# Second layer's scans: four of sixteen states turned in place of two, with a second tile of scaled copies and new tables by step

## The chip, the core and the metric

The kernel runs on one core of a Trainium2 chip. The core has a matrix engine (TensorE, in profiles PE for its matmuls and PEld for its weight loads), three engines that work on 128 partitions side by side (VectorE, DVE; ScalarE, ACT; GpSimd, POOL), and a queue that issues DMAs (SyncE, SP). Each runs its own instructions in order and waits for the others by semaphores. The metric is the device time of one execution in microseconds (us), lower is better. The kernel before takes 8835.18 us, the median of three runs (8833.89 to 8835.39).

## What is computed

The program is four layers on a tensor of 2 x 56 x 56 x 128. The change touches the second alone. It splits the 128 channels into four heads of 32 and works through them one after the other, since each head takes the result of the one before as input. The core of a head is a selective scan in four directions:

```
def _selective_scan(xs, dts, A, Bs, Cs, Ds):
    def step(h, inp):
        x_t, dt_t, B_t, C_t = inp
        dA = jnp.exp(dt_t[..., None] * A)
        h = dA * h + (dt_t * x_t)[..., None] * B_t[:, :, None, :]
        y = jnp.einsum('bkdn,bkn->bkd', h, C_t)
        return (h, y)
...
x1 = xx.reshape(B, L, d)
x2 = xx.transpose(0, 2, 1, 3).reshape(B, L, d)
xs = jnp.stack([x1, x2, jnp.flip(x1, 1), jnp.flip(x2, 1)], axis=1)
x_dbl = jnp.einsum('bkld,kcd->bklc', xs, p['x_proj_w'])
dts, Bs, Cs = jnp.split(x_dbl, [DT_RANK, DT_RANK + D_STATE], axis=-1)
```

Here L = 3136 pixels, d = 64 channels, n = 16 states. For each direction, channel and state there is a recurrence over the pixels: h = exp(delta A) h + (delta x) B, and the output sums h C over the 16 states. B and C do not depend on the channel, only on pixel and state; delta (after a softplus) and x do not depend on the state.

## The kernel before, in words

Both images lie side by side: 2 x 64 channels fill the 128 partitions. The pixels of one direction are cut into four quarters of 784 (`QT`), which makes 4 x 4 = 16 groups in a head. A group has 16 steps, one for each state, so a head has 256 steps and the layer 1024. Class `Scans` does this for both layers, with a table of settings from each; the first layer has 1024 steps of the same size in two runs of 512.

One step for state n of a group is:

- `decay` (L381): ACT computes a = exp(A delta).
- the input (delta x) B, in one of three ways. A **direct** state: PE spreads the row of B over all partitions into a PSUM tile named `b` (`spread`, L407, two bf16 matmuls), and DVE multiplies it by `du` = delta x (L479). A **pooled** state: DMAs copy the row to all partitions and POOL multiplies (L498). A **turned** state: `du` has been transposed once a group into `duT` (pixels on the partitions, `turn`, L237), and there B of a pixel is one number of a partition. ACT writes 7 x 2 scaled copies of `duT` for a state (`fan`, L359: seven blocks of 112 pixels, two images) into a tile bT, and PE transposes the seven blocks back into PSUM (`back`, L370).
- `scan` (L401): DVE runs the recurrence over the 784 pixels.
- POOL multiplies h by the row of C, which DMAs have copied to all partitions (p, L495), and PE adds p into the sum in PSUM, `acc` (`add_up`, L421).

For direct and pooled states a lies in PSUM, in one of two slots that the steps take by turns, and h in SBUF. For turned states it is the other way round: a lies in SBUF, and the input takes the slot. So the exponential of step s+1 waits for the scan of step s-1, whose slot it takes, unless s+1 is turned; that one is issued a step earlier still.

The order of all instructions is written out by hand. `emit(s)` issues for step s: ACT's `decay` of s+1 (if not turned), the copy of the state of s-1, `decay` of s+2 if turned, and the scaled copies that stand for s; PE's `back` of s+1; DVE's direct product of s+1; PE's `spread` of s+2; the prepared pieces; DVE's `scan` of s; the DMAs for C of s+3 and for B of s+6 if pooled; POOL's product p of s and, if s+3 is pooled, its input; and PE's additions. Three tables say how much of what stands at which step:

- `adds`: how many additions PE issues at a step, by the step modulo 32.
- `fans`: how the 14 scaled copies of a turned state are dealt out over the six steps before it; the key is the state's step modulo 32.
- `lists`: the pieces that prepare the next two groups during the 32 steps of the present pair, as (offset, place, name). The steps of a pair are counted 16 to 47, so a piece of offset 4 stands at step 20. `short` is the same for the first group of a head (steps 0 to 15, some pieces a little later), in which the groups 1 and 2 are prepared. All groups but the first go in pairs.

The pieces: `rows` (PE, then an ACT copy) projects x; `keep` and `fetch` send the rows to DRAM and back by SP's queue; `band` (ACT) and `rest` (POOL, L202) split the values of B into three bf16 parts; `store` and `spread` bring those by SP's queue to where PE reads them; `across` transposes B for the turned states (PE, ACT); `steps` (PE, ACT) and `soft` (ACT's softplus, which needs another table of functions than the exponential, so that ACT loads tables twice around it) give delta; `copy` (ACT) puts x into PSUM and `times` (DVE, L231) makes `du` from it; `turn` (PE, ACT) makes `duT`. `rows`, `steps`, `across`, `turn` and `copy` use the same single PSUM tile `b` as `spread`; each user waits until the one before has been read.

SP's queue also issues all DMAs for the rows of C and B, in the order of the program. The places in memory that matter: bT and the two `duT` lie in `big[5]`, each 896 columns wide. `big[0]` and `big[1]` are the halves of one tile, `pair`; in this layer `big[0]` holds the gate and the first 1792 columns of `big[1]` hold `prev`, the running result between heads. `run` of the layer runs the scans of a head, then the work between heads.

The tiles for turned states are handed out by turns:

```
self.duT, self.bT = w["turn"][0:2], w["turn"][2:]
...
for i, x in enumerate(x for x in steps if x["n"] in self.turned):
    x["bT"] = self.bT[i % len(self.bT)]
...
def direct(self, x):
    return x["n"] not in self.pooled and x["n"] not in self.turned
```

Of the kernel before, what the change touches and what calls it, by code (L numbers as in the profile page):

```python
# [21 lines left out]
B = 2  # L22
# [3 lines left out]
TP = 112  # L26
NT = L // TP
# [7 lines left out]
class Chip:  # L35


    def __init__(self, ctx, tc):
        self.tc, self.nc = tc, tc.nc
        nc = tc.nc  # L40
        const = ctx.enter_context(tc.tile_pool(name="const", bufs=1))
        self.ident = const.tile([128, 128], F32, name="ident")
        make_identity(nc, self.ident)
        self.eps = const.tile([128, 1], F32, name="eps")
        nc.gpsimd.memset(self.eps, 1e-5)
        self.one = const.tile([128, 1], F32, name="one")
        nc.gpsimd.memset(self.one, 1.0)
        self.ones = const.tile([1, 128], F32, name="ones")
        nc.gpsimd.memset(self.ones, 1.0)
        self.X = const.tile([TP, NT, B, C], F32, name="X")  # L50
        self._turn = 0
# [56 lines left out]
TS = QT // TP  # L108
# [469 lines left out]
def negative_exp(nc, t):  # L578
    nc.scalar.activation(t, t, AF.Exp)
    nc.vector.tensor_scalar_mul(t, t, -1.0)  # L580
# [19 lines left out]
def load(nc, pool, ap, name):  # L600
    t = pool.tile(list(ap.shape), F32, name=name)
    nc.sync.dma_start(t, ap)
    return t
# [232 lines left out]
class Layer1:  # L836
# [4 lines left out]
    D = 32  # L841

    def __init__(self, k, ctx, d, big):
        nc, tc = k.nc, k.tc
        D = self.D
        self.k = k
        wp = ctx.enter_context(k.pool("w1", side="right"))
        W = self.W = {n: load(nc, wp, d["L1_" + n], "L1" + n) for n in (
            "in_w", "taps", "conv_b", "dtb", "A", "Ds", "onw", "onb", "out_w")}

        xp = wp.tile([128, 4, 128], F32, name="xp1")
        dt = wp.tile([128, 4, 128], F32, name="dt1")
        nc.gpsimd.memset(xp, 0.0)
        nc.gpsimd.memset(dt, 0.0)
        for b in range(B):
            r, c = 34 * b, NS * b
            for i in range(2):
                o = r + 2 + NS * i
                nc.sync.dma_start(xp[:, :, 32 * i + c : 32 * i + c + NS], d["L1_xproj"][:, :, o : o + NS])
            nc.sync.dma_start(xp[:, :, 96 + 2 * b : 98 + 2 * b], d["L1_xproj"][:, :, r : r + 2])  # L860
            nc.sync.dma_start(dt[96 + 2 * b : 98 + 2 * b], d["L1_dt"][r : r + 2])
        sel = selection(k, wp, 2)
        R = self.R = {}
        for n in ("vss_skip", "cvm_skip", "final_ln_w", "final_ln_b"):
            t = wp.tile([TP, d["L1_" + n].shape[0]], F32, name="L1" + n)
            nc.sync.dma_start(t, d["L1_" + n].partition_broadcast(TP))
            R[n] = t
        nc.vector.tensor_scalar_add(R["vss_skip"], R["vss_skip"], 1.0)
        negative_exp(nc, W["A"])
        self.diag = wp.tile([128, 9, 128], F32, name="diag1")  # L870
        diagonals(k, self.diag, W["taps"])

        center = wp.tile([128, 128], F32, name="center1")
        nc.gpsimd.memset(center, 0.0)
        nc.gpsimd.memset(center[0:64, 0:64], 1.0 / 64)
        nc.gpsimd.memset(center[64:128, 64:128], 1.0 / 64)
        nc.vector.tensor_tensor(center, k.ident, center, ALU.subtract)
        skip = skips(k, wp, W["Ds"].unsqueeze(2), 1, center)
        self.mean = wp.tile([128, 2], F32, name="mean1")
        nc.gpsimd.memset(self.mean, 0.0)  # L880
        for b in range(B):
            nc.gpsimd.memset(self.mean[64 * b : 64 * (b + 1), b : b + 1], 1.0 / 64)
        self.outs = []
        for n in ("onw", "onb"):
            t = wp.tile([128, B * D], F32, name="out" + n)
            nc.vector.tensor_scalar(t, W["out_w"], W[n], None, ALU.mult)
            self.outs.append(t)

        lnw = wp.tile([B * D, 2], F32, name="lnw")
        for b in range(B):  # L890
            for i, n in enumerate(("ln1_w", "ln1_b")):
                nc.sync.dma_start(lnw[D * b : D * (b + 1), i : i + 1], d["L1_" + n].rearrange("(c o) -> c o", o=1))
        inb = self.inb = wp.tile([128, 2], F32, name="inb")
        with k.pool("pinb", psum=True) as pp:
            ps = pp.tile([128, 2], F32, name="pinb")
            for i in range(2):
                nc.tensor.matmul(ps[:, i : i + 1], lhsT=W["in_w"][:, i, :], rhs=lnw[:, 1:2], start=True, stop=True)
            nc.vector.tensor_copy(inb, ps)
        nc.vector.tensor_scalar(W["in_w"], W["in_w"], lnw[:, 0:1], None, ALU.mult)
        self.prev = big[1][:TP, 0 : NT * B * D].rearrange("p (j b c) -> p j b c", b=B, c=D)  # L900
        self.z, self.row, self.col, self.y = (big[i][:, 0:L] for i in (0, 2, 4, 3))
        self.scans = Scans(k, ctx, 1, [self.row], [self.col], [self.y], {
            "xproj": lambda kd, ci: xp[:, kd, :],
            "dt": lambda kd, ci: dt[:, kd, :],
            "dtb": lambda kd, ci: W["dtb"][:, kd : kd + 1],
            "A": lambda kd, ci, n: W["A"][:, kd, n : n + 1],
            "selB": lambda n: sel[:, n],
            "unused": sel[:, 0:4].rearrange("p n c -> p (n c)"),
            "skip": lambda ci: skip[:, 0],
            "sum": center,  # L910
            "rows": 64,
            "rowC": 32,
            "copies": (0, NS),
            "parts": ((0, 64, 0), (64, 128, NS)),
            "pooled": (1, 6, 9, 14),
            "turned": (3, 11),
            "adds": (0, 2, 2, 0, 0, 1, 2, 1, 1, 1, 1, 2, 1, 1, 1, 0, 3, 1, 0, 0, 0, 1, 2, 1, 1, 1, 2, 0, 1, 1, 1, 1),
            "soon": False,
            "fans": {
                None: (0, 4, 4, 4, 2, 0),  # L920
                3: (0, 10, 4, 0, 0, 0),
                11: (4, 0, 1, 7, 2, 0),
                19: (4, 5, 5, 0, 0, 0),
                27: (5, 1, 3, 2, 3, 0),
            },
            "lists": [
                [
                    (1, 0, "rows", [0, 1]), (2, 2, "keep"), (4, 0, "steps", 0, [0, 1]), (5, 2, "fetch"),
                    (9, 0, "across"), (9, 2, "band", 0), (9, 2, "rest", 0), (10, 2, "band", 1),
                    (10, 2, "rest", 1), (11, 2, "band", 2), (17, 2, "soft", 0), (19, 2, "store"),  # L930
                    (22, 2, "spread"), (23, 0, "copy", 0), (23, 2, "times", 0), (25, 0, "turn", 0),
                ],
                [
                    (12, 0, "rows", [0, 1]), (14, 2, "keep"), (15, 0, "steps", 0, [0, 1]), (17, 2, "soft", 0),
                    (19, 2, "fetch"), (20, 0, "across"), (27, 2, "band", 0), (27, 2, "rest", 0),
                    (28, 0, "copy", 0), (28, 2, "times", 0), (29, 2, "band", 1), (29, 2, "rest", 1),
                    (31, 2, "band", 2), (33, 2, "store"), (35, 2, "spread"), (39, 0, "turn", 0),
                ],
            ],
            "short": [  # L940
                [
                    (1, 0, "rows", [0, 1]), (4, 2, "keep"), (4, 0, "steps", 0, [0, 1]), (5, 2, "fetch"),
                    (6, 2, "soft", 0), (7, 0, "across"), (7, 2, "band", 0), (7, 2, "rest", 0),
                    (7, 2, "times", 0, False), (8, 2, "band", 1), (8, 2, "rest", 1), (9, 2, "band", 2),
                    (9, 2, "store"), (10, 2, "spread"), (12, 0, "turn", 0),
                ],
                [
                    (1, 0, "rows", [0, 1]), (1, 2, "keep"), (4, 0, "steps", 0, [0, 1]), (6, 2, "soft", 0),
                    (7, 0, "across"), (10, 2, "fetch"), (14, 2, "band", 0), (14, 2, "rest", 0),
                    (17, 2, "band", 1), (17, 2, "rest", 1), (19, 2, "band", 2), (20, 2, "store"),  # L950
                    (21, 2, "times", 0, False), (23, 0, "turn", 0), (24, 2, "spread"),
                ],
            ],
            "turn": [
                big[5][:TP, 128 * TS * i : 128 * TS * (i + 1)].rearrange("p (i c) -> p i c", c=128) for i in range(3)
            ],
        }, side="right")

# [1261 lines left out]
```

## Time and profile before

| what | value |
|---|---|
| median of three runs | 8835.18 us |
| the profiled execution, its own time | 8835.43 us |
| its span, first to last instruction | 8833.6 us |
| first layer's scans, two runs of 512 steps | 1184.6 and 1179.8 us |
| second layer's scans, four heads of 256 steps | 638.7, 638.4, 636.6, 636.6 us |
| busy over the whole span: PE, DVE, ACT, POOL | 8003.9, 6756.2, 5217.6, 6844.0 us |
| mean granted clock of TensorE | 0.958 |

The four heads' scans are 2550 us of the span, 29%. The rest (the first layer, the work between heads, both later layers) holds none of the changed instructions. For the whole program the slices of the page show which engine is busy when; each digit is the busy share of a fortieth of the span (221 us) in tenths:

```profile
DVE  8999998999987997998899799821266676665442
ACT  6888876888876776776777677533322222214331
POOL 5999986999986996998799699666577767756551
```

The second layer's heads are the thirteenth to the twenty-sixth slice; the digits that fall to 5 to 7 in DVE's row there are the stretches between heads. In a stretch of scans DVE, POOL and PE are all busy most of the time, so the slices cannot say which of them sets the pace. That is read from the table by stretch, and from what each engine's idle time waited for. In those lines a group reads: line, engine, operation, what it writes and reads, shapes, count | busy us, mean ns of one | idle time of the engine just before them, and who ended it.

### The profile page before, as it was taken

The page shows a single profiled execution, that of the slowest core. Times are in us where ns is not written, and L with a number is a line of the kernel's source. Part 1 is how long each engine was busy: PE and PEld are TensorE (multiplying, and loading weights), DVE is VectorE, ACT ScalarE, POOL GpSimd, SP SyncE. Part 2 cuts the span into 40 slices and gives each one's busy share as a digit, 9 for nine tenths or more (in the row PEclk, how much of TensorE's full clock was granted, in tenths as well). Part 3 has the DMA queues.
Part 4 walks back from the last instruction along what each step waited for, and adds up shares of the span by engine and source line. Part 5 has one row for each costly group of instructions (what it writes and reads, how often), then busy time and mean ns, then how long its engine had stood idle before and what let it go on. Part 6 is the DMA issues. An engine that isn't in the chain of part 4 may idle for free. (4 is left out here: it accounts for less than half of the span.)

```text
span 8833.6 us, 103494 instructions
## 1 busy us (share of the span) xinstructions
PE 8003.9 (91%) x31559; PEld 4877.1 (55%) x31559; DVE 6756.2 (76%) x7017; ACT 5217.6 (59%) x11166; POOL 6844.0 (77%) x4232
## 2 busy tenths in 40 slices
PE   8999999999998888888888888699989989989998
PEld 4555555555554444444444444345578878875555
DVE  8999998999987997998899799821266676665442
ACT  6888876888876776776777677533322222214331
POOL 5999986999986996998799699666577767756551
PEclk9999999999998999999899899799999999989999
DMA  4676654667654884885688488320133333320004
GB/s 145 217 218 213 211 186 128 217 217 213 211 179 109 221 219 118 215 223 161 173 224 216 116 224 219 93 34 3 30 98 106 103 93 106 104 56 8 15 1 139
DMA packets 846617, 1276.69 MB, mean 145 GB/s; under 512 B 182813, under 2 KB 504350, under 8 KB 846058
## 3 DMA queue, kind: packets, MB, share of 16 engines
q1 hardware_dynamic: 846058, 1270.07, 50.7%
q8 instruction: 249, 4.08, 0.2%
q14 instruction: 310, 2.54, 0.1%
HBM read 1230.00 MB, written 46.58 MB: 145 GB/s over the span
## 5 line engine op out<-in xcount | busy, mean ns | idle before, releaser
L495 POOL TENSOR_TENSOR p<-h,c 128x784 f32<-128x784 f32 x2048 | 3763.7, 1864 | 291.8 <-DVE h L401 146.0
L401 DVE TENSOR_TENSOR_SCAN h<-a,state,h 128x784 f32<-128x784 f32 x1200 | 2169.9, 1833 | 2.5 <-ACT a L381 1.6
L421 PE MATMUL acc<-p,center 128*128 128x392 f32 x4096 | 1496.8, 501 | 6.5 <-POOL p L495 6.3
L421 PE MATMUL acc<-p,ident 128*128 128x392 f32 x4096 | 1429.5, 493 | 0.5 <-POOL p L495 0.4
L479 DVE TENSOR_TENSOR h<-du,b 128x784 f32<-128x784 f32 x1152 | 1096.5, 952 | 229.7 <-PE b L407 212.5
L381 ACT ACTIVATE a<-delta,L1A 128x784 f32<-128x784 f32 x896 | 819.8, 915 | 425.0 <-DVE h L401 418.6
L421 PEld LDWEIGHTS acc<-p,ident 128*128 128x128 f32 x4096 | 747.6, 190 | 533.4 <-issue 33.4
L421 PEld LDWEIGHTS acc<-p,center 128*128 128x128 f32 x4096 | 743.0, 193 | 497.1 <-issue 25.0
L1232 POOL TENSOR_TENSOR total<-total,e 128x448 f32<-128x448 f32 (+1 forms) x644 | 734.6, 1141 | 329.1 <-ACT e L1221 289.6
L498 POOL TENSOR_TENSOR h<-du,b 128x784 f32<-128x784 f32 x448 | 831.7, 1857 | 0.0
L1221 ACT ACTIVATE e<-sc 128x448 f32<-128x448 f32 (+1 forms) x700 | 376.9, 542 | 722.8 <-PE sc L1219 594.6
L407 PE MATMUL b<-three,sel 96*128 96x512 bf16 (+1 forms) x2304 | 587.0, 336 | 174.0 <-DVE h L479 102.0
L381 ACT ACTIVATE a<-delta,L0A 128x784 f32<-128x784 f32 x704 | 643.3, 914 | 169.7 <-DVE h L401 165.2
L401 DVE TENSOR_TENSOR_SCAN h<-a,h 128x784 f32<-128x784 f32 x400 | 702.6, 1774 | 3.5 <-ACT a L381 3.1
L359 ACT ACTIVATE X<-X,BT 112x128 f32<-112x128 f32 x2100 | 683.8, 391 | 0.2
L1736 POOL TENSOR_TENSOR u<-u,T 128x1024 f32<-128x1024 f32 x192 | 448.6, 2358 | 265.9 <-DVE u L1734 265.7
L401 DVE TENSOR_TENSOR_SCAN h<-h,state,a 128x784 f32<-128x784 f32 x336 | 618.0, 1839 | 0.0
L1720 ACT ACTIVATE less<-cv 128x512 f32<-128x512 f32 x256 | 152.1, 595 | 612.2 <-PE cv L1698 586.9
L407 PEld LDWEIGHTS <-sel 96*128 96x128 bf16 x2304 | 225.0, 101 | 521.3 <-issue 365.5
L359 ACT ACTIVATE big<-big,BT 112x64 f32<-112x64 f32 x1680 | 444.6, 335 | 0.0
L1732 ACT ACTIVATE T<-T 128x1024 f32<-128x1024 f32 x128 | 135.2, 1056 | 407.4 <-DVE T L1730 279.2
L1837 PE MATMUL pj<-u,Wm 128*128 128x196 f32 (+8 forms) x1536 | 355.6, 385 | 21.2 <-POOL u L1756 11.1
(541 smaller groups left out, 14336.4 us busy)
## 6 DMA issues: line engine op xcount, KB each, us to landing
c<-rows SPq DMA_DIRECT2D x1024, 392.0 KB, 4.0
c<-rows SPq DMA_DIRECT2D x2048, 196.0 KB, 4.0
b<-rows SPq DMA_DIRECT2D x512, 196.0 KB, 4.6
b<-rows SPq DMA_DIRECT2D x192, 392.0 KB, 4.6
wA<-win SPq DMA_DIRECT2D x64, 448.0 KB, 3.9
wB<-win SPq DMA_DIRECT2D x64, 448.0 KB, 6.2
wC<-win SPq DMA_DIRECT2D x64, 448.0 KB, 4.7
wD<-win SPq DMA_DIRECT2D x64, 448.0 KB, 3.8
```

Source lines behind the costliest of these rows:

```text
L359: self.k.nc.scalar.activation(x["bT"][:, i, c0:c1], g["duT"][x["ci"]][:, i, c0:c1], AF.Copy, scale=g["BT"][:, r : r + 1])
L381: self.k.nc.scalar.activation(x["a"], g["delta"][ci], AF.Exp, scale=self.w["A"](g["kd"], ci, x["n"]))
L401: self.k.nc.vector.tensor_tensor_scan(h, a, b, start, ALU.mult, ALU.add)
L407: self.k.nc.tensor.matmul(ps[:, c0:c1], lhsT=self.w["selB"](x["n"]), rhs=x["g"]["three"][:, c0:c1], start=True, stop=True)
L421: nc.tensor.matmul(job["acc"][:, i, 0:392], lhsT=self.w["sum"], rhs=x["p"][:, 392 * i : 392 * (i + 1)], start=False, stop=n == NS - 1,)
L479: nc.vector.tensor_tensor(one["h"], one["g"]["du"][one["ci"]], one["b"], ALU.mult)
L495: nc.gpsimd.tensor_tensor(now["p"], now["h"], now["c"], ALU.mult)
L498: nc.gpsimd.tensor_tensor(three["h"], three["g"]["du"][three["ci"]], three["b"], ALU.mult)
L1221: nc.scalar.activation(e[:n], ps[:n], AF.Exp, scale=scale)
L1232: nc.gpsimd.tensor_tensor(total[:n], total[:n], e[:n], ALU.add)
L1736: nc.gpsimd.tensor_tensor(u[:, :, :, o], u[:, :, :, o], half, ALU.add)
L1837: nc.tensor.matmul(ps[:, lo - c0 : hi - c0], lhsT=Ws[f][:, eo, 3 - r, :], rhs=u[:, b, f, lo - a0 : hi - a0], start=f == 0, stop=f == 1,)
```

## The change

In the second layer's settings the states 7 and 15 join 3 and 11 as turned ones; the pooled ones stay, so eight of sixteen are direct where ten were. A fourth tile is added to `turn`, in the free columns of `big[1]` behind `prev`, so that there are two bT by turns. The tables `adds`, `fans`, `lists` and `short` are new; the pieces are the same, at other steps. No function is changed.

```diff
             "pooled": (1, 6, 9, 14),
-            "turned": (3, 11),
-            "adds": (0, 2, 2, 0, 0, 1, 2, 1, 1, 1, 1, 2, 1, 1, 1, 0, 3, 1, 0, 0, 0, 1, 2, 1, 1, 1, 2, 0, 1, 1, 1, 1),
+            "turned": (3, 7, 11, 15),
+            "adds": (2, 0, 2, 0, 2, 0, 1, 3, 0, 2, 1, 1, 1, 0, 1, 2, 1, 1, 0, 0, 0, 1, 2, 1, 1, 1, 1, 2, 1, 0, 1, 1),
             "soon": False,
             "fans": {
                 None: (0, 4, 4, 4, 2, 0),
-                3: (0, 10, 4, 0, 0, 0),
-                11: (4, 0, 1, 7, 2, 0),
-                19: (4, 5, 5, 0, 0, 0),
-                27: (5, 1, 3, 2, 3, 0),
+                3: (1, 10, 1, 1, 1, 0),
+                7: (3, 9, 0, 2, 0, 0),
+                11: (1, 0, 0, 13, 0, 0),
+                15: (6, 2, 2, 4, 0, 0),
+                19: (0, 6, 0, 4, 4, 0),
+                23: (2, 2, 7, 3, 0, 0),
+                27: (1, 6, 3, 2, 2, 0),
+                31: (0, 5, 5, 4, 0, 0),
             },
             "lists": [
                 [
-                    (1, 0, "rows", [0, 1]), (2, 2, "keep"), (4, 0, "steps", 0, [0, 1]), (5, 2, "fetch"),
-                    (9, 0, "across"), (9, 2, "band", 0), (9, 2, "rest", 0), (10, 2, "band", 1),
-                    (10, 2, "rest", 1), (11, 2, "band", 2), (17, 2, "soft", 0), (19, 2, "store"),
-                    (22, 2, "spread"), (23, 0, "copy", 0), (23, 2, "times", 0), (25, 0, "turn", 0),
+                    (1, 0, "rows", [0, 1]), (5, 0, "steps", 0, [0, 1]), (6, 2, "keep"), (11, 2, "fetch"),
+                    (12, 0, "across"), (15, 2, "band", 0), (15, 2, "rest", 0), (17, 2, "band", 1),
+                    (17, 2, "rest", 1), (20, 2, "band", 2), (21, 2, "store"), (22, 2, "soft", 0),
+                    (23, 0, "copy", 0), (23, 2, "times", 0), (25, 2, "spread"), (28, 0, "turn", 0),
                 ],
                 [
-                    (12, 0, "rows", [0, 1]), (14, 2, "keep"), (15, 0, "steps", 0, [0, 1]), (17, 2, "soft", 0),
-                    (19, 2, "fetch"), (20, 0, "across"), (27, 2, "band", 0), (27, 2, "rest", 0),
-                    (28, 0, "copy", 0), (28, 2, "times", 0), (29, 2, "band", 1), (29, 2, "rest", 1),
-                    (31, 2, "band", 2), (33, 2, "store"), (35, 2, "spread"), (39, 0, "turn", 0),
+                    (13, 0, "rows", [0, 1]), (15, 0, "steps", 0, [0, 1]), (17, 2, "keep"), (22, 2, "fetch"),
+                    (22, 2, "soft", 0), (26, 2, "band", 0), (26, 2, "rest", 0), (29, 0, "across"),
+                    (31, 2, "band", 1), (31, 2, "rest", 1), (31, 0, "copy", 0), (31, 2, "times", 0),
+                    (33, 2, "band", 2), (36, 2, "store"), (40, 2, "spread"), (41, 0, "turn", 0),
                 ],
             ],
             "short": [
                 [
-                    (1, 0, "rows", [0, 1]), (4, 2, "keep"), (4, 0, "steps", 0, [0, 1]), (5, 2, "fetch"),
-                    (6, 2, "soft", 0), (7, 0, "across"), (7, 2, "band", 0), (7, 2, "rest", 0),
-                    (7, 2, "times", 0, False), (8, 2, "band", 1), (8, 2, "rest", 1), (9, 2, "band", 2),
-                    (9, 2, "store"), (10, 2, "spread"), (12, 0, "turn", 0),
+                    (1, 0, "rows", [0, 1]), (1, 2, "keep"), (3, 2, "fetch"), (5, 0, "across"),
+                    (5, 2, "band", 0), (5, 2, "rest", 0), (6, 2, "band", 1), (6, 2, "rest", 1),
+                    (7, 0, "steps", 0, [0, 1]), (9, 2, "band", 2), (9, 2, "store"), (10, 2, "spread"),
+                    (10, 2, "soft", 0), (11, 2, "times", 0, False), (13, 0, "turn", 0),
                 ],
                 [
-                    (1, 0, "rows", [0, 1]), (1, 2, "keep"), (4, 0, "steps", 0, [0, 1]), (6, 2, "soft", 0),
-                    (7, 0, "across"), (10, 2, "fetch"), (14, 2, "band", 0), (14, 2, "rest", 0),
-                    (17, 2, "band", 1), (17, 2, "rest", 1), (19, 2, "band", 2), (20, 2, "store"),
-                    (21, 2, "times", 0, False), (23, 0, "turn", 0), (24, 2, "spread"),
+                    (5, 0, "rows", [0, 1]), (6, 2, "keep"), (9, 2, "fetch"), (9, 0, "steps", 0, [0, 1]),
+                    (10, 2, "soft", 0), (12, 2, "band", 0), (12, 2, "rest", 0), (14, 2, "band", 1),
+                    (14, 2, "rest", 1), (14, 2, "times", 0, False), (15, 0, "across"), (23, 2, "band", 2),
+                    (23, 2, "store"), (23, 0, "turn", 0), (25, 2, "spread"),
                 ],
             ],
             "turn": [
-                big[5][:TP, 128 * TS * i : 128 * TS * (i + 1)].rearrange("p (i c) -> p i c", c=128) for i in range(3)
+                t[:TP, at : at + 128 * TS].rearrange("p (i c) -> p i c", c=128)
+                for t, at in [(big[5], 128 * TS * i) for i in range(3)] + [(big[1], NT * B * D)]
             ],
```

## The prediction, made before the changed kernel was run

> **What bounds the kernel now.** I read the page first: the chain of waits stops after one step (0%), so it says nothing, and the busy shares (PE 91%, POOL 77%, DVE 76%) mix stages. The change touches only the second layer's scans, so the table by stretch comes next, one row for each of the four heads, from its first scan to its last:
>
> ```profile
> core 0: us, PE busy (x) PEld busy (x) DVE busy (x) ACT busy (x) POOL busy (x), PEclk, DMA share, GB/s
> ...
> 2768.82:3407.54 638.72, 549.27 (x1952) 296.28 (x1951) 604.37 (x430) 461.33 (x1060) 594.15 (x349) 0.94 0.80 215
> 3503.69:4142.12 638.43, 548.37 (x1952) 295.19 (x1951) 604.43 (x430) 461.42 (x1060) 596.53 (x350) 0.95 0.80 212
> 4239.57:4876.21 636.64, 548.00 (x1952) 296.15 (x1951) 604.27 (x430) 461.42 (x1060) 594.63 (x349) 0.94 0.80 213
> 4973.51:5610.10 636.59, 547.83 (x1952) 296.16 (x1951) 604.22 (x431) 461.39 (x1060) 594.81 (x350) 0.94 0.79 213
> ```
>
> Mean head 637.6 us: DVE busy 604.3 (95%), POOL 595.0 (93%), PE 548 (86%), ACT 461 (72%). The groups by line for DVE, and the waits of POOL, both in the second head alone:
>
> ```profile
> L401 DVE TENSOR_TENSOR_SCAN h<-a,state,h 128x784 f32<-128x784 f32 x168 | 303.2, 1835 | 0.8 <-POOL h L498 0.8
> L479 DVE TENSOR_TENSOR h<-du,b 128x784 f32<-128x784 f32 x159 | 151.3, 952 | 33.2 <-PE b L407 31.7 <-POOL p L495 0.4
> ```
> ```profile
> POOL p L495 <- PE acc L421: 13.2, 11, 2.0
> POOL p L495 <- DVE h L401: 11.6, 14, 5.3
> ```
>
> DVE's whole idle time in a head (33 us) stands before its direct products and ends with b, the rows that PE spreads into the one PSUM tile `b`. No scan waits for ACT, while ACT itself waits 105 us a head for scans. So DVE sets the pace, its only loss is the shared tile, and POOL has 42 us to spare. Scan starts in this head give 52.0 us for the first group of 16 steps, 42.1 for the second and (4142.1 - 3597.8)/14 = 38.9 for each other. The first group's direct products alone wait 13.7 us; there two later groups are prepared in 16 steps.
>
> Durations on the page include a tail that overlaps the next instruction. For sums I use the distance of starts, read off the order of time in the second head:
>
> ```profile
> 3593.85 2.24 ACT L359 ACTIVATE big<-big,BT 112x64 f32<-112x64 f32 x9
> 3601.55 1.28 ACT L221 ACT_TABLE_LOAD   x1
> 3602.84 1.61 ACT L221 ACTIVATE delta<-delta 128x784 f32<-128x784 f32 x2
> ```
> ```profile
> 3599.54 0.94 DVE L479 TENSOR_TENSOR h<-du,b 128x784 f32<-128x784 f32 x1
> 3600.40 3.58 DVE L401 TENSOR_TENSOR_SCAN h<-a,state,h 128x784 f32<-128x784 f32 x2
> ```
> ```profile
> 3602.30 0.89 PE L370 MATMUL a<-ident,big 112*128 112x112 f32 x7 [0.26 <-DVE h L401]
> 3603.03 0.50 PE L407 MATMUL b<-three,sel 96*128 96x512 bf16 x2
> ```
>
> One product 0.86 us (3600.40 - 3599.54), one scan 1.75, one scaled copy 0.24 (nine in 2.24 less one tail), seven transposes 0.73, one spread 0.33 to 0.5. POOL's starts are 1.81 apart, and its small subtraction takes 0.5.
>
> **The change, part by part.** Per head there are 16 groups. The 32 steps of a pair of groups are counted 16 to 47, as in the tables; those of the first group 0 to 15.
>
> 1. States 7 and 15 are turned instead of direct. DVE loses 2 products a group: 32 x 0.86 = 27.5 us, leaving 577. Its scans stay: with a in SBUF and b in PSUM one takes 1839 ns against 1835. The range of this term is the tail's: 0.86 to 0.95, 27.5 to 30.5; I take starts.
>
> 2. ACT gains 28 scaled copies a group: 448 x 0.24 = 107 us, so 461 + 107 = 568; ACT goes from 72% to 93% of a head. It is hidden only if it lies in ACT's 105 us of waiting for scans, and that cover is now used up.
>
> 3. PE loses 32 spreads (11 to 16 us) and gains 32 sets of seven transposes (23 us): +10 net, 558. The Trainium skill ("TensorE: Matmul & The Clock Gate", Part 4: PE-mode transpose) gives about 275 ns for one transpose inside a kernel. That would be 7 x 0.275 = 1.9 us a set, +45 us a head, and PE would reach 593, level with POOL. The row says 0.10 each when they follow each other (0.73 for seven); I take the row.
>
> 4. POOL's instructions stay the same: 16 + 4 products and two subtractions a group, 20 x 1.81 + 2 x 0.5 = 37.2. **So the floor of a head is POOL's 595**, not DVE's 577: at most 42.6 of 637.6 can be won, 170 us over four heads.
>
> 5. The second tile of copies lies in `pair`, where only the gate and `prev` live; in the scans nobody else touches those. Turned steps are now four apart instead of eight and copies begin six steps ahead, so with one tile they would wait for the transposes; with two, tile by turns, they do not. Cost 0.
>
> 6. The preparation moves. `rows` stays at step 17 (n=1), where the next direct product is n=4; it cost about 0.5 us and will again. `steps` at 20 had two scans (3.5 us) before the next direct product, n=7. Now it stands at 21 and the next is n=8, three scans on (5.2 us). `across` and the second `rows` at 28 and 29 also have three scans: 0.6 + 0.3 + 1.6 + 0.8 + 0.5, some 4 us with handoffs. Of the mean 1.3 us of waiting a group outside the first (19.5/15), I keep 0.4. In the first group the two `rows` no longer meet at step 1, but `across` and a `rows` share step 5.
>
> 7. SP's queue: `keep`, `fetch`, `store` and `spread` move with their DMAs; each waits for data and holds up the c rows queued behind. c is issued three steps (some 7 us) ahead and lands after 4.0. `fetch` now stands 2 to 5 steps behind `keep` (1 to 9 before), `spread` 1 to 4 behind `store` (1 to 4 before). I count 0 (bounds: +3 to -6 us a head, the latter being all that POOL waits for c there).
>
> 8. Where ACT may be late. Steps 38 to 43 carry it all: two softplus with two table loads (1.6 + 2 x 1.29 = 4.2 us) at 38, `copy` at 39, thirteen copies at 40, six at 41. Clock from the end of scan 37. State 7 is turned and its exponential was issued at 37, so the softplus run 0.1 to 4.3, and decay 40 ends at 5.2. DVE does scan 38, one product, scan 39 by 4.4, then wants `times`, which needs `copy`, queued behind decay 40: 6.0. DVE waits 1.6 to 2. Then ACT: decay 41 by 7, thirteen copies by 10.1, decay 42 by 11; DVE, after `times`, scan 40, a product and scan 41, stands at about 11.2. No more than 0.3 is lost. So some 2 us in 32 steps, 1 a group. The Trainium skill ("ScalarE: Activation LUTs", What ACT_TABLE_LOAD costs) puts a switch of tables at 2.66 us, a drain of 1.38 included. That is 2.8 us more here, paid in full by DVE because nothing covers it. The trace has load, softplus, softplus at 3601.55, 3602.84 and the next load at 3604.55, with no drain between; I take 1.29.
>
> **Sum.** In a later group DVE needs 37.6 - 1.7 = 35.9, + 0.4 (tile) + 1 (ACT) = 37.3; POOL 37.2. POOL's products end 2 to 4 us behind their scans, so a DVE wait of 2 us is mostly eaten by POOL's backlog. For what is not, the nearest row is the first layer's scans: there the bound engine, DVE, stands idle 41 us in 32 groups, 1.3 each; I take half, 0.6, between 0 and 1.3. Group: 37.2 + 0.6 = 37.8, 14 of them 529. Second group 42.1 to 38.3. First group: DVE 36.7, two handoffs of about 1.2, and ACT with 13 us of work in steps 8 to 10 against DVE's 6, of which 5 are not covered: 44 in place of 49.5 to 52. Head 611.5, saving 26.1, over four heads 104. Against the profiled execution's own time (8835.4; the median 8835.2 is the same) that gives **8731 us**.
>
> **Rivals.**
> - *Likeliest (0.66): POOL is the bound, with small waits.* 8731; own range 8690 to 8775, from 0.1 to 1.2 us of waits a group.
> - *POOL's floor (0.08).* All waits hide, a head takes 598: 8677. For it: POOL's backlog. Against: the first group starts without one.
> - *Half given back (0.12).* PE, ACT, DVE and POOL are all near 90% and run in order, so new handoffs arise: group 38.6, first 46, second 40; saving 10.6 a head: 8793. For it: the two steady states so far lie 1.3 us a group above their busiest engine (first layer 37.0 over DVE's 35.75, here 38.9 over 37.6).
> - *Slower (0.10): ACT becomes the bound.* Place: the exponential of the next step but one is queued behind the copies and may not run ahead, since its PSUM slot comes free only with a scan. If nothing carries over from step to step, 32 steps cost the sum of the larger of ACT's and DVE's work in each. With the counts of the tables ACT is over DVE by 2.4 us at step 38, 2.3 at 40, 1.3 at 17, 1.1 at 21, 1.0 at 29, 0.9 at 19, and 3.0 in nine others: 71.7 + 12.0 = 84 us against 77.8 now: 3.1 a group worse, 14 x 3.1 = 43 a head, less about 3 in the first: 8995. It decides from 6 us of ACT waits in 32 steps (77.8 - 71.7). Against: the same sum for before is 82, though no scan waited for ACT.
> - *No effect (0.04)*: the released time turns into waits for b; direct products fall from 10 to 8 in 16, so this needs twice the wait for each.
>
> **Numbers.** This kernel can be told from unchanged beyond 0.2% (18 us). Faster 0.84, within 0.05, slower 0.11. The range 8675 to 8812 leaves out the slower cases and the floor's tail.
>
> **What would show it.** L479 x1024 and L359 x5824 in all; DVE busy near 577 a head, ACT near 568, POOL still 595; POOL at 97% of a head. Waits of L479 for b under 15 us a head. Waits of scans for ACT at 40 to 42, and of `times` for its copy. Wrong, if scans wait for ACT more than 3 us a group, or POOL idles over 30 us a head.

## The result, and the profile after

The changed kernel takes 8764.12 us, median of four runs (8756.58 to 8767.42), beside 8835.28 us for the kernel before: a ratio of 0.9919, with a 95% interval of 0.9907 to 0.9931. Run again later beside the last experiments it took 8746.5 against 8830.81, a ratio of 0.9906 (0.9892 to 0.9921). So it is faster by 0.8 to 0.9%: 71 and 84 us. The forecast was 104 us won, in a range of 23 to 160.

The table by stretch, first scan to last scan of each head, for the changed kernel:

```profile
core 0: us, PE busy (x) PEld busy (x) DVE busy (x) ACT busy (x) POOL busy (x), PEclk, DMA share, GB/s
2768.55:3384.71 616.16, 544.69 (x2106) 303.86 (x2106) 575.10 (x398) 562.75 (x1509) 593.79 (x349) 0.98 0.85 223
3483.85:4101.52 617.67, 547.52 (x2105) 305.75 (x2105) 575.48 (x398) 563.10 (x1509) 593.61 (x349) 0.97 0.85 220
4200.64:4814.57 613.93, 546.34 (x2106) 305.01 (x2106) 575.73 (x398) 563.11 (x1509) 593.38 (x349) 0.97 0.85 221
4912.17:5528.45 616.28, 546.02 (x2106) 305.19 (x2106) 575.60 (x399) 562.78 (x1509) 595.32 (x351) 0.97 0.85 220
```

A head takes 616.0 us on average in place of 637.6. DVE's busy time fell by 29 us to 575, ACT's rose by 102 to 563, PE's stayed at 546, POOL's at 594. POOL is now busy 96% of a head, where DVE was at 95%. Over four heads that is 86.4 us won, of which the profile's span shows 73.6 (8833.6 to 8760.0); the other 13 us were lost outside the scans, see below.

Scan starts put the first group of a head at 45.5 to 46.3 us (49.5 to 52.0 before), the second at 37.4 to 39.4 (41.8 to 42.1), each later one at 38.0 (39.0, both the mean of the four heads).

What DVE waited for in the second head (engine and line that waited, who ended it, total us, times, longest):

```profile
DVE h L479 <- PE b L407: 22.2, 23, 2.7
DVE h L401 <- POOL h L498: 15.4, 16, 1.8
DVE du L231 <- ACT b L225: 3.2, 5, 0.8
```

And what POOL waited for there:

```profile
POOL p L495 <- DMA c<-rows: 10.3, 10, 2.6
POOL p L495 <- DVE h L401: 5.4, 4, 2.3
POOL p L495 <- PE b L173: 3.9, 2, 2.1
```

Two things are new. Scans now wait for POOL's inputs of pooled states (15 us, 0.8 before): DVE runs into POOL's backlog. And POOL's largest wait in this head is for rows of C from DMA; before, it was for PE and DVE. This head has the most of it: over the four heads the rows of C come to 6.9 us a head (4.4 before), about as much as POOL's waits for scans (6.7), while POOL's whole idle time fell from 43 to 22 us. No scan waits for ACT in any amount worth a line.

### The profile page after: what moved, and what is told of

It is laid out like the page before. It is cut to its first block, busy times and chain, and to the rows that moved or that the text cites. A ratio compares the mean times of both kernels' runs of the same rounds, so it can differ in the third digit from the quotient of the medians.

```text
span 8760.0 us, 106320 instructions
## 1 busy us (share of the span) xinstructions
PE 8013.3 (91%) x32199; PEld 4929.5 (56%) x32199; DVE 6642.9 (76%) x6889; ACT 5622.6 (64%) x12956; POOL 6845.1 (78%) x4232
## 5 line engine op out<-in xcount | busy, mean ns | idle before, releaser
L401 DVE TENSOR_TENSOR_SCAN h<-a,state,h 128x784 f32<-128x784 f32 x1104 | 1993.7, 1834 | 29.5 <-POOL h L498 27.2
L479 DVE TENSOR_TENSOR h<-du,b 128x784 f32<-128x784 f32 x1024 | 976.9, 954 | 192.5 <-PE b L407 175.5
L381 ACT ACTIVATE a<-delta,L1A 128x784 f32<-128x784 f32 x768 | 700.9, 913 | 148.3 <-DVE h L401 144.2
L401 DVE TENSOR_TENSOR_SCAN h<-h,state,a 128x784 f32<-128x784 f32 x432 | 795.4, 1841 | 0.0
L381 ACT ACTIVATE a<-delta,L0A 128x784 f32<-128x784 f32 x704 | 643.0, 914 | 169.8 <-DVE h L401 164.4
L401 DVE TENSOR_TENSOR_SCAN h<-a,h 128x784 f32<-128x784 f32 x368 | 644.3, 1775 | 29.5 <-POOL h L498 24.0
L407 PE MATMUL b<-three,sel 96*128 96x512 bf16 (+1 forms) x2048 | 516.1, 333 | 100.2 <-DVE h L479 42.7
L1725 ACT ACTIVATE less<-cv 128x512 f32<-128x512 f32 x256 | 152.2, 595 | 611.5 <-PE cv L1703 586.2
L359 ACT ACTIVATE pair<-big,BT 112x64 f32<-112x64 f32 x1680 | 444.0, 337 | 0.0
L407 PEld LDWEIGHTS <-sel 96*128 96x128 bf16 x2048 | 198.1, 100 | 319.9 <-issue 214.1
```

Source lines behind the costliest of these rows:

```text
L359: self.k.nc.scalar.activation(x["bT"][:, i, c0:c1], g["duT"][x["ci"]][:, i, c0:c1], AF.Copy, scale=g["BT"][:, r : r + 1])
L381: self.k.nc.scalar.activation(x["a"], g["delta"][ci], AF.Exp, scale=self.w["A"](g["kd"], ci, x["n"]))
L401: self.k.nc.vector.tensor_tensor_scan(h, a, b, start, ALU.mult, ALU.add)
L407: self.k.nc.tensor.matmul(ps[:, c0:c1], lhsT=self.w["selB"](x["n"]), rhs=x["g"]["three"][:, c0:c1], start=True, stop=True)
L479: nc.vector.tensor_tensor(one["h"], one["g"]["du"][one["ci"]], one["b"], ALU.mult)
L1725: nc.scalar.activation(turned, self.product(2 * j, pairs), AF.Copy, scale=float(1 + j))
```

## The experiments

Each was compared by the length of its four heads in its own profile, since the rest of the program moves by some 10 us from run to run; where runs were timed, the median of four executions is given too. The kernels no_pool6, half_copies, c5, early, early2 and before_c5 were executed once. Two profiles of the changed kernel gave heads of 616.0 and 615.7 us on average.

### Which part does it: the turned states or the lists?

Two kernels take one half of the change each. The first has only the new `lists` and `short`; the second has all but these:

```diff
 # lists_only, against the kernel before
 "turned": (3, 11),
 "lists": [
     [
-        (1, 0, "rows", [0, 1]), (2, 2, "keep"), (4, 0, "steps", 0, [0, 1]), (5, 2, "fetch"),
+        (1, 0, "rows", [0, 1]), (5, 0, "steps", 0, [0, 1]), (6, 2, "keep"), (11, 2, "fetch"),
...
 # old_lists, against the changed kernel
 "turned": (3, 7, 11, 15),
 "lists": [
     [
-        (1, 0, "rows", [0, 1]), (5, 0, "steps", 0, [0, 1]), (6, 2, "keep"), (11, 2, "fetch"),
+        (1, 0, "rows", [0, 1]), (2, 2, "keep"), (4, 0, "steps", 0, [0, 1]), (5, 2, "fetch"),
...
```

> The kernel before with the new lists and short list alone; turned states, adds, fans and tiles stay. Theory (the gain comes from the two products taken off DVE; the lists only make room for it): states 7 and 15 are direct here, so steps at 21 meets a direct product again; later groups 38.5 to 40 us (38.9 before), first group 45 to 50 (50.4 before), heads 630 to 642 us (637.6 before), the whole within 30 us of before. Rival (the lists are most of the gain, since they keep the preparation out of the way of the tile b): heads 626 us or less, 45 us or more won in all.

> The changed kernel with the lists and the short list of before. Theory: DVE is busy 575 us a head as in the changed kernel, the first group is near 50 us as before, and later groups lose some to ACT, because both softplus at step 33 now meet four copies there and nine at 34; heads 619 to 630 us (616.0 changed, 637.6 before). Rival (without the new lists the freed products turn into waits): heads 634 us or more.

Measured: lists_only 9132.57 us (ratio 1.0338, 1.0323 to 1.0354), heads 710.6 to 712.8; old_lists 9038.62 us (1.0232, 1.0215 to 1.0249), heads 679.9 to 685.5. Both are far slower than either kernel, and I had both sizes wrong; only the rival of old_lists (the freed products turn into waits, 634 us or more) was right in kind. DVE's waits in the second head of lists_only:

```profile
DVE h L479 <- PE b L407: 88.2, 48, 5.0
DVE du L231 <- ACT b L225: 16.0, 11, 2.4
```

and of old_lists:

```profile
DVE h L479 <- PE b L407: 65.1, 52, 3.1
DVE h L401 <- ACT a L381: 21.4, 14, 2.6
DVE h L401 <- ACT state L392: 9.8, 4, 5.5
```

Read by step, lists_only waits 4.05 us behind the scan of step 22 (nothing there in the kernel before): `steps` at 21 now stands between two spreads of direct states, and DVE's product of state 8 must sit through it.

In old_lists DVE has the smaller load of the changed kernel (581 us busy) and still a head takes 45 us more than in the kernel before. Both softplus stand at step 33 there, with copies around them, and the exponential of step 36 comes 2.4 us too late for its scan. The product of state 8, three steps on, waits 3.0 us for `b`, but no piece in `b` holds it up. The order of time on PE in the second head shows what does:

```profile
3739.43 2.98 PE L435 MATMUL acc<-big,ident 128*128 128x392 f32 x4 [2.66 <-ACT big L441]
3742.21 3.69 PE L421 MATMUL acc<-p,center 128*128 128x392 f32 x8
3745.73 0.84 PE L370 MATMUL a<-ident,pair 112*128 112x112 f32 x7
3746.41 0.50 PE L407 MATMUL b<-three,sel 96*128 96x512 bf16 x2
```

PE stands until ACT, late behind the softplus, has taken the last sum out of `acc` (L441). Then it begins the next sum, adds, transposes, and only then comes to the spread of state 8. This wait of PE at step 36 is 2.7 us on average in 16 of the 28 pairs of groups and 3.7 in the other 12; in the changed kernel it is 0.6 and 1.4. The product of state 12 waits 1.4 us behind `turn` at step 41.

Neither half is worth anything alone. The turned states open gaps of three scans in the use of the tile `b`; the new lists put the long pieces into just those gaps, and both softplus at another step. With four turned states these lists are worth 45 + 21.6 = 67 us a head; which of the moved pieces carries how much was not separated. Neither theory holds as stated. (The tables of `adds` and `fans` stayed on the side of the turned states in both.)

### Which engine sets the pace now?

One kernel takes work from POOL, one from ACT. In no_pool6 the product of du and B is left out for one state; in half_copies the second image's scale is left out:

```diff
 # no_pool6, against the changed kernel
-        if three and three["n"] in self.pooled:
+        if three and three["n"] == 6 and self.nch == 1:
+            three["h"] = three["b"]
+        elif three and three["n"] in self.pooled:
...
 # half_copies, against the changed kernel
-            "parts": ((0, 64, 0), (64, 128, NS)),
+            "parts": ((0, 128, 0),),
```

> The changed kernel, but for pooled state 6 of the second layer POOL's product of du and B is left out and the scan takes the row of B as it is: one POOL instruction of 1.81 us less in each group (29 us a head), nothing else. Theory (POOL sets the pace of the later groups): the waits of scans for POOL's h (11 to 15 us a head) go and heads fall by 8 to 16 us, to 600 to 608, where DVE's 575 and its waits for the tile b take over. Rival ACT (the copies and softplus set the pace): less than 4 us a head. Rival DMA (rows of C land too late): less than 6 us a head, and waits of POOL for c stay at 10 us or more.

> The changed kernel, but a block's copy is made for both images at once with the first image's B (the second image's scale is left out): 7 copies of 128 columns for a turned state in place of 14 of 64, so ACT has about 5 us less in a group (some 85 us a head). Theory (POOL sets the pace): the waits of times for its copy (3 us a head) and a part of the waits for b go, but POOL's 594 us stay; heads fall by 2 to 8 us. Rival ACT: heads fall by 14 us or more.

Measured: no_pool6 heads 608.9, 613.7, 610.6, 610.6, mean 611.0, which is 5.1 less; half_copies 614.3, which is 1.7 less. The second head of each by stretch, no_pool6 first:

```profile
3474.76:4088.45 613.69, 547.33 (x2105) 306.26 (x2105) 574.52 (x398) 562.83 (x1509) 566.82 (x333) 0.97 0.80 221
```
```profile
3488.23:4102.39 614.16, 545.04 (x2106) 305.18 (x2106) 575.78 (x398) 486.42 (x1067) 593.99 (x349) 0.97 0.82 221
```

ACT lost 77 us of work in a head (563 to 486) and the head hardly moved. The 1.7 us are no more than the kernel early below shows (1.8) in groups that its edit does not touch, and DVE's wait for the copy of x, which was to go, stayed at 3.1 us. ACT at 91% is not the bound, and the slower rival of the prediction is refuted. POOL lost 27 us and the head gave back 5. The waits that POOL's relief removed came back elsewhere, as DVE's waits in the second head of no_pool6 show:

```profile
DVE h L479 <- PE b L407: 29.6, 27, 3.1
DVE du L231 <- ACT b L225: 7.4, 4, 2.3
DVE h L401 <- POOL h L500: 0.9, 2, 0.8
```

The wait for POOL is gone (15.4 to 0.9; the line is L500 in this kernel), that for b is up by 7 and that for the copy of x by 4. So POOL sets the pace, but DVE with its waits for `b` stands only some 5 us a head behind it. The theory named the order rightly and put too much distance between the two: the 8 to 16 us were not reached. The rival DMA asked for less than 6 us and for waits for c of 10 us or more. These were 5.8 to 10.8 us in the four heads, 8.4 on average, so this run alone does not rule out that late rows take part. (The edit also holds the tile of the row of B until p has read it; SP's waits for POOL in the second head did not grow by that, 198 us against 202.)

### The rows of C

POOL's largest wait in the second head is for the rows of C. A row's DMA can be issued only when one of four tiles is free again, that is, after an earlier product p. This edit adds a fifth tile in the second layer, first to the changed kernel, then to the kernel before:

```diff
-        self.cp = ctx.enter_context(k.pool("scanc", 4))
+        self.cp = ctx.enter_context(k.pool("scanc", 4 if nch == 2 else 5))
```

> The changed kernel with five tiles for the rows of C in place of four in the second layer, so that SP can ask for a row one product of POOL earlier. Theory (POOL sets the pace and loses up to 10 us a head to rows of C that land late): those waits fall under 3 us and heads by 3 to 8 us, to 608 to 613. Rival (the 16 DMA engines are full, 85% busy here, and a row asked for earlier lands no earlier): heads within 2 us of 616, waits for c stay.

> The changed kernel with five tiles for the rows of C in the second layer, now timed. Theory: heads 609 to 612 as in the look before, 16 to 26 us less than the changed kernel in all. Rival (that look was a lucky one): within 8 us of the changed kernel.

> The kernel before with five tiles for the rows of C in the second layer. Theory (late rows cost time only once POOL sets the pace; before, POOL has 42 us to spare in a head): heads 635 to 638 us, as before (637.6), though POOL's waits for c shrink. Rival (late rows cost the same in both kernels, so the tile is an improvement of its own): heads 630 to 633.

Measured: in the changed kernel, heads of 610.5 on average in both profiles, 5.5 less, all of it in the later groups (37.97 to 37.53 us); timed, 8734.18 us (ratio 0.989 to before, 0.9874 to 0.9907), 12 us under the changed kernel beside it. Heads agree with the theory; the median is less than the 16 us it asked for, with the two ranges 0.6 us apart (8728.92 to 8738.61 and 8739.17 to 8766.95). POOL's waits in the second head of the timed kernel:

```profile
POOL p L495 <- DVE h L401: 4.9, 4, 2.3
...
POOL p L495 <- DMA c<-rows: 1.7, 3, 0.8
```

The rival is refuted: at the same busy share of the DMA engines, 0.85, an earlier request helps. By the starts in the traces, a row is requested 7.0 us on average before the product that uses it in the changed kernel and 9.1 us with the fifth tile, and it lands after 4.6 us (median; 7.5 at most).

That the whole 5.5 us are late rows is not shown. In this head POOL's wait for them fell by 8.6 us, the most of the four; on average it fell from 6.9 to 4.1 us (to 3.0 in the other profile), where under 3 was expected. In the later groups of a head POOL's idle time fell from 10.0 to 4.1 us: its waits for rows from 3.0 to 0.9, for scans from 3.4 to 1.3, for additions from 2.1 to 0.8. The last two can follow from late rows, since scans and additions wait for POOL in their turn; but the tile also lets SP go on to the DMAs that stand behind the rows of C in its queue, and no run separates the two. Nor is POOL alone the limit now. A later group takes 37.5 us here with 37.2 of POOL's work, and 37.6 in no_pool6 with 35.4.

In the kernel before, POOL's wait for c in the second head, without and with the fifth tile:

```profile
POOL p L495 <- DMA c<-rows: 6.6, 3, 3.6
```
```profile
POOL p L495 <- DMA c<-rows: 2.7, 4, 1.0
```

This head differs the most here too: over the four heads the wait is 4.4 us a head without the tile and 4.3 with it. The heads go from 637.6 to 635.9 on average, in one execution. About 0.9 of these 1.7 us lie in the later groups (38.95 to 38.88), the rest in first groups, which differ from head to head by more. So the tile that is worth 5.5 us a head once POOL is the bound is worth at most 1.7 before.

### The first group of a head

The first group prepares two groups in 16 steps and is 8 us longer than the others. Three edits tried to shorten it: another table of copies for ACT (early), besides that two pieces a step earlier (early2, and early2_c5 with the fifth tile), and other additions (c5_adds, with the fifth tile):

```diff
 # early
-            at = self.w["fans"]
+            at = self.w["fans"] if x["s"] >= NS else self.w.get("early", self.w["fans"])
...
+                7: (0, 8, 4, 2, 0, 0),
+                11: (0, 6, 4, 4, 0, 0),
+                15: (0, 0, 6, 5, 3, 0),
 # early2, besides
-                    (1, 0, "rows", [0, 1]), (1, 2, "keep"), (3, 2, "fetch"), (5, 0, "across"),
+                    (1, 0, "rows", [0, 1]), (1, 2, "keep"), (3, 2, "fetch"), (4, 0, "across"),
...
-                    (5, 0, "rows", [0, 1]), (6, 2, "keep"), (9, 2, "fetch"), (9, 0, "steps", 0, [0, 1]),
+                    (4, 0, "rows", [0, 1]), (6, 2, "keep"), (9, 2, "fetch"), (9, 0, "steps", 0, [0, 1]),
...
 # c5_adds
-        for _ in range(self.adds[s % len(self.adds)]):
+        adds = self.w.get("first_adds", self.adds) if s < NS else self.adds
+        for _ in range(adds[s % len(adds)]):
...
+            "first_adds": (0, 0, 0, 0, 2, 0, 2, 1, 1, 1, 2, 1, 1, 1, 1, 1),
```

> The changed kernel with a table of its own for the copies of the first group: at most eight at a step in place of thirteen, none at steps 9 and 10, where steps and both softplus stand, and one in place of four at step 1 before the copy of rows. Theory (in the first group PE's pieces wait in b because ACT stands in copies and softplus): its waits for b fall from 7 to 8.5 us to 4 to 6, the group from 46 to 43 to 44.5 us; later groups unchanged; heads 614 or less. Rival (the pieces themselves are too many for the first group, whatever ACT does): the first group stays within 1 us.

> As early, and across and the second rows stand at step 4 in place of 5, ahead of PE's start of a sum and its additions there (three scans of room before the next direct product), turn at 12 in place of 13. Theory (PE reaches these pieces too late because 5 us of matmuls of step 4 stand before them): the wait before the product of state 8 (2.1 us at step 6) goes under 0.7, the first group to 41.5 to 43.5. Rival (three scans are too short for both pieces anyway): no better than early.

> Both together: new places in the first group and a fifth tile for the rows of C. Theory: the savings add, 3 to 4.5 us in the first group and 3 to 8 in the rest of a head; heads 604 to 610, 8715 to 8745 in all (8764 changed). Rival (DMA full): 8745 to 8755.

> Five tiles for the rows of C, and additions dealt out anew in the first group of a head (two, one, one at steps 6 to 8 in place of one, three, none; 14 to step 15 as before). Theory (in the first group the spread for state 10 waits behind three additions of step 7, on a TensorE whose granted clock is low at the start of a head): the wait at step 8 (2.2 to 2.7 us) falls under 1.5, the first group from 46 to 44.5 to 45.5, heads to 608 to 611. Rival (the chain of steps, its ACT copy and the spread is the limit): no change against c5_timed.

Measured: early leaves the first group at 45.2 to 46.4 us (heads 614.2 on average; the 1.8 us less lie in the other groups, which the edit does not touch); early2 makes it 48.8 to 49.9 (heads 618.5), and early2_c5 48.8 to 54.0 (8743.8 us, heads 614.7). All three missed what their theories said of the first group. To deal out ACT's copies otherwise does not help, and the two pieces at step 4 hold up more than they free: a scan there waits 2.7 us for ACT, which stands behind the copy of the second `rows`. c5_adds did what was asked at step 8 (wait 2.6 to 1.2 us) and lost it again one to three steps on; first group 46.3 to 47.4, second 36.7 in place of 37.4 and 39.3, heads 610.2. At 8726.27 us (0.9884, 0.9869 to 0.9898) it has the lowest median of all, but its range (8725.81 to 8740.03) overlaps c5_timed's, and its heads are the same within 0.3 us; a gain over the fifth tile alone is not shown.

The profile shows something else that none of these edits touches. The order of time on PE at the start of the second head of the changed kernel, and the stretches of 10 us there:

```profile
3486.56 2.98 PE L173 MATMUL b<-big,xp 128*128 128x392 f32 x4 [2.20 <-DVE h L479]
...
3499.38 1.58 PE L173 MATMUL b<-big,xp 128*128 128x392 f32 x4 [0.43 <-ACT BT L237]
```
```profile
3483.85:3493.85 10.00, 6.72 (x19) 3.77 (x19) 8.34 (x6) 7.68 (x21) 6.15 (x4) 0.57 0.36 87
3493.85:3503.85 10.00, 9.34 (x38) 5.34 (x37) 7.74 (x7) 6.26 (x15) 8.99 (x6) 0.92 0.82 203
```

The same four matmuls of `rows` take 2.98 us at a granted clock of 0.57 and 1.58 us at 0.92. PE enters this head at little more than half its clock. A comparison of heads bounds what that costs: the second and third head of the changed kernel have 0.57 in their first 10 us and a first group of 46.3 us; the first and last head have 0.83 there and 45.5 us. So some 0.8 us of the 8 go with the clock. No run set it by itself, and the cause of the rest stays open.

### Time lost outside the scans

13 us of the profile's difference lie outside the heads: the stretches between heads took 295.9 us after (290.9 before), and the stretch behind the last head 3231.6 (3223.5).

> The changed kernel as it is, beside the next two on the same chip. Heads 613 to 618 us; the time 8755 to 8768. The stretch behind the last head, which no edit touches, took 3223.5 us in the profile of before and 3231.6 in that of the changed kernel; if the difference belongs to the clock and not to the change, it comes out anywhere between 3222 and 3232 again.

Measured: heads 615.7 on average, the stretch behind the last head 3231.9 us. Over all profiles of this study it took 3222.1 to 3231.9, for kernels with the same instructions there: 3222.1 in c5_timed and 3229.7 in c5, which are the same kernel. The lines show what differs. In the last layer, a stretch of 10 us of the kernel before and then of the changed one, each beginning 1 to 2 us ahead of the same sums:

```profile
8665.00:8675.00 10.00, 9.95 (x77) 9.52 (x75) 4.08 (x7) 0.00 (x0) 2.66 (x1) 0.86 0.11 41
```
```profile
8586.00:8596.00 10.00, 9.94 (x47) 9.62 (x47) 1.73 (x3) 0.00 (x0) 2.66 (x1) 0.50 0.04 15
```

PE is busy in both, but does 77 matmuls in one and 47 in the other, at a granted clock of 0.86 and 0.50. In the order of time, the sums there read, before and after:

```profile
8667.06 4.17 PE L1999 MATMUL sum<-selT,X 112*128 112x64 f32 x32
```
```profile
8587.10 7.09 PE L2004 MATMUL sum<-selT,X 112*128 112x64 f32 x32
```

By the clock's own records it stayed at half for 30.7 us there in place of 20.5. That happens in some profiles and not in others, of kernels with the same instructions there: from the first of these sums to the end of the program, five profiles with 20.5 us took 166.6 to 166.9 us and nine with 30.7 took 171.7 to 173.3. Here that makes 6.3 of the 8.1 us, and the 8 us are not shown to be an effect of the change. Where the rest of the scatter arises stays open.

Of the 5 us between heads, 1.4 in each of the three stretches appear with the change already at the end of the head: ACT takes the last sum out of `acc` 5.3 us behind the last scan in place of 3.9. POOL's last product ends 3.6 us behind that scan in place of 2.2, which fits. But in no_pool6 it ends after 3.2 us and the sum is taken out no earlier (5.4), so the cause stays open.

## Why the prediction was right in direction and in its range, and 33 us too low

- **The bound, and the floor.** Right. DVE set the pace before; POOL's unchanged instructions do after (594 us forecast 595; 96% of a head, forecast 97%). The floor held.
- **Part 1, DVE.** 27.5 us forecast, 29 measured in busy time.
- **Part 2, ACT.** 107 us forecast, 102 measured. It was hidden whole: even 77 us less of it gained no more than 1.7, which is within what such profiles differ by.
- **Part 3, PE.** +10 us forecast, -2 measured. The row of the trace (0.73 us for seven transposes) was the one to take. By the estimate from the 275 ns of the Trainium skill ("TensorE: Matmul & The Clock Gate", Part 4: PE-mode transpose) PE would have reached 593; it was busy 546. The granted clock, higher in these heads (0.97 or 0.98, before 0.94 or 0.95), is large enough to make the step from 558 to that (558 x 0.9425 / 0.9725 = 541, an estimate from the means of the tables).
- **Part 5, the second tile.** No wait on it shows; a run with one tile was not made.
- **Part 6, the preparation.** The waits for b were taken too low: 13.7 us outside the first group in the second head where about 6 were forecast, and 22 in the whole head, over the 15 that were to be a sign. And the step misjudged what the lists are worth: it treated them as a correction of under 1 us a group, and they decide the sign. Without them the four turned states lose 45 us a head.
- **Part 7, the rows of C.** This is the term that was mis-sized most: counted as 0 with bounds of +3 to -6 a head, the four tiles for these rows cost 5.5 us a head, 22 over four. The mean distances were right (7.0 us from request to use, 4.6 to landing); the step left out the late ones (up to 7.5 us). It took the 6.6 us of waits in one head of before as what could be won, and missed that a wait of an engine with room to spare is free there and counts once that engine is the bound. Requests also come later: POOL's products, which free the tiles, start 1.6 us behind the end of their scans in place of 1.0.
- **Part 8, ACT late at steps 38 to 43.** The wait of `times` for its copy is there, 0.43 us on average in 32 steps, where 1.6 to 2 were forecast. DVE comes to it late, having waited for POOL before the scan of step 38 (1.2 us), and that covers a part: in no_pool6, where this wait is gone, the wait for the copy rises to 1.0 us. Scans did not wait for ACT at steps 40 to 42. A table load costs 1.29 us, as the row has it: in the second head of the changed kernel one starts at 3514.83, the softplus behind it at 3516.12. The drain of 1.38 us more that the Trainium skill counts ("ScalarE: Activation LUTs", What ACT_TABLE_LOAD costs) does not appear.
- **The sum.** First group 45.9 forecast 44; second 38.5 forecast 38.3; later ones 38.0 forecast 37.8: 616.0 a head, forecast 611.5. That is 18 us of the miss in the profile; the other 13 are the stretches outside the heads, 6.3 of them with the clock of the last layer. With the fifth tile the head is 610.5, close to the forecast, but partly by luck: there the first group is 2.2 us longer than forecast, the second 0.6, and the fourteen later ones together 3.8 us shorter.
- **The rivals.** Most like the likeliest, a third of the way to "half given back" (21.6 us saved a head, between 26.1 and 10.6). The groups that this second rival names, 46 + 40 + 14 x 38.6, make 626.4 us, a saving of 11.2 and not 10.6; nothing else rests on it.

## What to carry to other kernels

Before you read an engine's wait as harmless, ask what it costs when that engine becomes the bound: a fifth tile for the rows of C was worth at most 1.7 us a head before POOL set the pace, and 5.5 after. Where pieces share one buffer with the main loop, the choice of which steps use that buffer and the places of the pieces are one decision; half of it made the kernel 2 to 3% slower. When four engines stand at 89 to 96%, the relief of one is worth little (27 us off POOL gained 5, 77 off ACT at most 2), since the next stands right behind it.

## What the runs showed of the hardware

- One place in the last layer, where TensorE's granted clock stays at half for 20.5 or for 30.7 us, moves the rest of the program by 5 to 7 us from one execution to the next.
- TensorE's mean granted clock over a head went from 0.94 or 0.95 to 0.97 or 0.98, though its busy time stayed the same; in the first 10 us of the changed kernel's heads it is 0.57 or 0.83.
- At a DMA share of 0.85 and 220 GB/s rows of 196 KB landed 4.6 us after issue (median of the four heads; 4.0 before, at 0.80), and with requests some 2 us earlier POOL's waits for them in the later groups fell from 3.0 to 0.9 us a head.
